# Reordering POOL's scatters, an earlier query copy and a few small copies in a sparse graph-network kernel

## The chip, the cores and the metric

The kernel runs on one core of one Trainium2 chip. The metric is the device time of one execution in microseconds, and lower is better. The kernel before took 2139.91 us, the median of three runs (2137.19 to 2143.26).

## The reference, cut to what matters

The program is a network of four graph layers on 1024 nodes with 16 batch entries of 128 features each. Layers 0, 2 and 3 are attention layers, layer 1 is a graph-attention layer without queries. About 8 of 1024 entries in each row of the adjacency matrix are set.

```python
def attention_layer(adj, h):              # layers L0, L2, L3
    Q, K, V = h @ Wq, h @ Wk, h @ Wv      # 8 heads of 16
    scores = einsum(Q, K) / sqrt(16)
    scores = where(adj == 0, -inf, scores)
    out = softmax(scores) @ V
    x = layer_norm(h + out @ Wo + bo, ln1_g, ln1_b)
    return layer_norm(x + relu(x @ W1 + b1) @ W2 + b2, ln2_g, ln2_b)

def graph_layer(x, adj):                  # layer L1
    h = x @ W
    e = leaky_relu((h @ a_src)[:, :, None] + (h @ a_dst)[:, None, :])
    att = softmax(where(adj == 0, -inf, e))
    return layer_norm(att @ h + x, ln_gamma, ln_beta)

x = L3(L2(L1(L0(x))))
```

## The kernel before

**What is computed how.** Because the graph is sparse, the kernel never builds the 1024 x 1024 scores. Its first 150 us or so turn the adjacency matrix into lists of neighbours. In each layer every node's keys and values are written as one row of a table in HBM, and a tile of 128 nodes then gathers the rows of its neighbours. The batch is cut into two groups (`g`) of eight entries, and the nodes into eight tiles (`t`) of 128, so that a layer has 16 "units" (`g`, `t`), and the program 64. `h` counts the two halves of a group.

**Parts.** A unit's neighbours are taken in chunks. One chunk is one indirect DMA of 128 rows (L968, in `gathered`). Chunks are grouped into parts. In attention layers a unit has five parts: four of two chunks and, in the fourth place, one of a single chunk, the *shared* chunk (`MIX` in the code), which collects what is left of the four groups of 32 nodes. A part's rows land in one of four gather buffers (`e`), and its gathers are put into the program four parts ahead (`AHEAD`), right after the last reader of that buffer.

**The work on a part**, for attention:

- VectorE multiplies the gathered keys by the expanded queries (L982, in `products`; 128 x 2048) and reduces over each head (L1015, in `exponentials`). ScalarE takes the exponential (L1019).
- VectorE multiplies the gathered values by the exponentials (L1043, in `weighted`). This is the last reader of the buffer `e`.
- TensorE sums the weighted rows by node, with a matrix of marks as the weights (L1059, in `marked`, called by `summed`).

For the shared chunk the first product is made by GpSimd (POOL) instead, in place, in the tile `qx` (L997, in `product_of_shared`). `qx` has a single buffer. Ahead of it `shared` copies to `qx` those rows of the expanded queries `qr` that the shared chunk needs, by two or three DMAs on SyncE's queue (SP, L946). The reduction L1015 and the product L1043 of that chunk then work on `qx`, and TensorE's sum reads it last.

**The end of a unit.** `divided` takes the sum of the exponentials (a matmul), VectorE divides (L1096, L1099), and two tails per unit (`attention_tail`, one for each half) do the output projection, the norms and the feed-forward part, mostly on TensorE and ScalarE. `finish` closes a tail. In layers L0 to L2 it stores the new state (`kept`, L575) and projects it to the next layer's table (L592, L617, L618), both by DMAs on SP. In L3 it transposes the result back into the tile `outs` on ScalarE (L660) and, after the second half, scatters it to the output by an indirect DMA on POOL (L699); the very last unit scatters its two halves separately (L693).

**The order.** The order of instructions is written out by hand; no scheduler moves them. The main loop goes over all parts. In one turn it emits, for part `i`: the product of part `i`, the sum of part `i - 2`, steps of the tails and of the next unit's queries (`others`), the scores and exponentials of part `i`, on the unit's second turn `shared(u)`, more `others`, the weighted rows of part `i - 1`, the gathers of part `i + 3`, and the product of the shared chunk of part `i + 2`. When a tail's steps come is set by a table of letters for each layer (`PLANS`), or by a pace. Each engine and each issuing queue works in the order in which it was given its instructions. In L3 a scatter comes out of one of the `others` of a unit's second turn, which puts it in POOL's queue ahead of the two gathers of the unit's last part, the product L997 and the sum of checks `seen` (L1112).

**Small weight parts.** `load_weights` loads an attention layer's weights and folds the mean and one bias into others: it subtracts a product of `W1` and `b2` from `b1` (L529, VectorE, from PSUM). `load_graph_weights` transposes the graph layer's weight matrix; VectorE copies the transpose `wgT` (L551) and two further columns (L555) out of PSUM.

```python
            if here and i == begun + 1:
                if is_attention(u):
                    shared(u)
...
                gathered(i - 1 + AHEAD)
                product_of_shared(i + 2)
```

Of the kernel before, what the change touches and what calls it, by code (L numbers as in the profile page):

```python
# [17 lines left out]
AF = mybir.ActivationFunctionType  # L18
ALU = mybir.AluOpType
# [4 lines left out]
D = 128  # L24
# [3 lines left out]
F = FF // P  # L28
# [117 lines left out]
def sparse_path(ctx: ExitStack, tc: tile.TileContext, a: dict, out: bass.AP, flag):  # L146


    nc = tc.nc
# [329 lines left out]
    w = {}  # L479
# [12 lines left out]
    def load_weights(layer):  # L492

        t = wts.tile([P, 2 * D], F32, tag="Wkv", name="Wkv")
        nc.sync.dma_start(t[:, :D], a[f"{layer}_gnn_Wk"])
        nc.sync.dma_start(t[:, D:], a[f"{layer}_gnn_Wv"])
        w[layer, "Wkv"] = t
        yield  # L500
        for name in ATTN:
            src = a[f"{layer}_gnn_{name}"]
            if name in ("Wq", "Wo", "W1"):
                t = wts.tile([P, src.shape[1]], F32, tag=name, name=name)
                nc.sync.dma_start(t, src)
            elif name == "W2":
                t = wts.tile([P, F, D], F32, tag=name, name=name)
                nc.sync.dma_start(t, src.rearrange("(f p) d -> p f d", p=P))
            elif name == "b1":
                t = wts.tile([P, F], F32, tag=name, name=name)  # L510
                with nc.allow_non_contiguous_dma(reason="a bias, once"):
                    nc.sync.dma_start(t, src.rearrange("(f p) -> p f", p=P))
            elif name.startswith("ln") or name in ("b2", "bo"):
                t = wts.tile([P, 1], F32, tag=name, name=name)
                nc.sync.dma_start(t, src.rearrange("(p o) -> p o", o=1))
            else:
                continue
            w[layer, name] = t
        yield
        centred(w[layer, "Wo"], D)  # L520
        centred(w[layer, "W2"].rearrange("p f d -> p (f d)"), F * D)
        ps = bank([P, F])
        for f in range(F):
            nc.tensor.matmul(
                ps[:, f : f + 1], w[layer, "W1"][:, f * P : (f + 1) * P], w[layer, "b2"],
                start=True, stop=True,
            )
        yield
        nc.vector.tensor_tensor(w[layer, "b1"], w[layer, "b1"], ps, ALU.subtract)  # L529
        nc.vector.tensor_tensor(w[layer, "ln1_b"], w[layer, "ln1_b"], w[layer, "b2"], ALU.add)  # L530

    wg = const.tile([P, D + 2], F32, name="wg")

    def load_graph_weights():
        for name in GAT[3:]:
            t = const.tile([P, 1], F32, name=name)
            nc.sync.dma_start(t, a[f"L1_gnn_{name}"].rearrange("(p o) -> p o", o=1))
            w["L1", name] = t

        nc.sync.dma_start(wg[:, :D], a["L1_gnn_W"])  # L540
        ends = const.tile([P, 2], F32, name="ends")
        for k, name in enumerate(("a_dst", "a_src")):
            nc.sync.dma_start(
                ends[:, k : k + 1], a[f"L1_gnn_{name}"].rearrange("(p o) -> p o", o=1)
            )
        yield
        ps = bank([P, P])
        nc.tensor.transpose(ps, wg[:, :D], ident)
        yield
        wgT = wts.tile([P, P], F32, tag="Wo", name="wgT")  # L550
        nc.vector.tensor_copy(wgT, ps)  # L551
        ps = bank([P, 2])
        nc.tensor.matmul(ps, wgT, ends, start=True, stop=True)
        yield
        nc.vector.tensor_copy(wg[:, D:], ps)  # L555
        centred(wg[:, :D], D)

    tables = {}
# [106 lines left out]
        return v.rearrange("p (o d) -> p o d", o=1).to_broadcast([P, GH, D])  # L665

    leaving = {}

    def finish(l, g, t, h, z, gain, shift, dve=False):
        if l + 1 < len(LAYERS):  # L670

            wanted[0] = True
            while held[0]:
                advance(slow)
            wanted[0] = False
            busy[0] += 1
            xn = states.tile([P, GH, P], F32, tag="xT", name="xT")
            turned(z, xn, gain, shift)
            yield "free"
            yield from project(l + 1, g, t, h, xn)  # L680
            busy[0] -= 1
            return
        xn = states.tile([P, GH, P], F32, tag="xT", name="xT")
        turned(z, xn, gain, shift, dve)
        yield
        if h == 0:
            leaving[g, t] = twos.tile([P, HF, GH, D], F32, tag="kv", name="outs")
        o = leaving[g, t]
        turned(xn, o[:, h], dve=dve)
        yield  # L690
        yield
        if (l, g, t) == units[-1]:
            nc.gpsimd.indirect_dma_start(  # L693
                out=out.rearrange("n (k c) -> (n k) c", k=GR * HF),
                out_offset=bass.IndirectOffsetOnAxis(ap=halves[:, h : h + 1], axis=0),
                in_=o[:, h].rearrange("p g d -> p (g d)"), in_offset=None,
            )
        elif h + 1 == HF:
            nc.gpsimd.indirect_dma_start(  # L699
                out=out.rearrange("n (k c) -> (n k) c", k=GR),  # L700
                out_offset=bass.IndirectOffsetOnAxis(ap=places[:, g, t : t + 1], axis=0),
                in_=o.rearrange("p h g d -> p (h g d)"), in_offset=None,
            )

    def hidden():
        return ones_.tile([P, F * GH * P], F32, tag="f1", name="f1")
# [168 lines left out]
    def is_attention(u):  # L875
        return LAYERS[units[u][0]][1] is ATTN
# [62 lines left out]
    def shared(u):  # L939

        qx[u] = queries_of_shared()
        of = [j for j, _ in QUARTERS[units[u][2]]]
        for j in sorted(set(of)):
            at = slice(32 * of.index(j), 32 * (S - of[::-1].index(j)))
            if of[: S].count(j) * 32 == at.stop - at.start:
                nc.sync.dma_start(qx[u][at], qs[u][at, j, :])  # L946
                continue
            for s in range(S):
                if of[s] == j:
                    at = slice(32 * s, 32 * s + 32)  # L950
                    nc.sync.dma_start(qx[u][at], qs[u][at, j, :])
# [36 lines left out]
    def product_of_shared(i):  # L988

        if i >= len(parts):  # L990
            return
        u, pieces = parts[i]
        if not is_attention(u) or (MIX, 0) not in pieces[0]:
            return
        own = qx[u].rearrange("p (o c) -> p o c", o=1)
        prs[i] = [own]
        nc.gpsimd.tensor_tensor(own, es[i][:, :1, :ROW], own, ALU.mult)  # L997
# [142 lines left out]
    def planned(beyond="abq"):  # L1140
        n = opening[0]
        opening[0] += 1
        for c in plan[0][n] if n < len(plan[0]) else beyond:
            if c == "q":
                aside()
                continue
            for gen in tails:
                if half_of[gen] == "ab".index(c):
                    step(gen, tails)
                    break  # L1150
# [4 lines left out]
    def others():  # L1155
        if opening[0] is not None:
            planned()
            for _ in range(eager[0]):
                advance(idle())
            return  # L1160
        pace[0] += pace[1]
        while pace[0] >= 1.0:
            advance(tails)
            pace[0] -= 1.0
        aside()
        for _ in range(eager[0]):
            advance(idle())
# [18 lines left out]
    with tc.manual_schedule():  # L1186
# [41 lines left out]
        begun = 0  # L1228
        for i in range(len(parts) + 2):
            here = i < len(parts)  # L1230
            u = parts[i][0] if here else len(units)
            if here:
                l = units[u][0]
                eager[0] = 1 if u < 2 else 0
                if i and parts[i - 1][0] != u:
                    begun = i
# [11 lines left out]
            if i > 1:  # L1248
                summed(i - 2)
                done = parts[i - 2][0]  # L1250
                if parts[i - 1 : i] == [] or parts[i - 1][0] != done:
                    closing = divided(done)
                    next(closing)
            others()
            if here:
                exponentials(i)
            if here and i == begun + 1:
                if is_attention(u):
                    shared(u)
                while loads:  # L1260
                    advance(loads)
                if u + 1 < len(units):
                    fronts.append(queries(u + 1))
                loads.append(loaded(u + 2))
                if u:
                    advance(loads)
            others()
            if 0 < i <= len(parts):
                weighted(i - 1, 0)
                if not is_attention(parts[i - 1][0]):  # L1270
                    others()
                    weighted(i - 1, 2)
                gathered(i - 1 + AHEAD)
                product_of_shared(i + 2)
                for _ in sizes:
                    pass
            if closing is not None and here:
# [25 lines left out]
                    advance(fronts)  # L1303
        while opening[0] < len(plan[0]):
            planned()
        while tails:
            advance(tails)
        for _ in closing:
# [438 lines left out]
```

## Time and profile before

| | |
|---|---|
| median of three runs | 2139.91 us |
| the profiled execution's own time | 2128.25 us |
| its span | 2126.4 us |
| TensorE (PE) busy | 1955.3 us (92%) |
| VectorE (DVE) busy | 1818.9 us (86%) |
| ScalarE (ACT) busy | 1516.5 us (71%) |
| GpSimd (POOL) busy | 1173.0 us (55%) |
| granted TensorE clock, mean | 0.973 |

The profile is of one execution. "Busy" is the time in which an engine ran an instruction; instructions that only issue a DMA on SP are not counted. A row of the groups gives the line, the engine, the operation, out<-in, the count, then the busy time, the mean of one in ns, and the idle time of the engine just ahead of it with what ended that idle time. A row of the waits gives who waited for whom, then the sum in us, the number of times and the longest. A row of the timeline gives start, length, engine, line and operation, and in brackets the idle time ahead of it. A row of the busy time by stage gives the stretch, its length, and for TensorE, its weight loads, VectorE, ScalarE and POOL the busy time and the number of instructions, then the granted clock, the busy share of the DMA engines and GB/s.

In time the program runs: lists of neighbours and first projections to about 130 us, layer L0 to about 660, L1 to about 1000, L2 to about 1530, L3 to about 2090, and the last two tails to 2126.4.

### The profile page before, as it was taken

The page shows a single profiled execution, that of the slowest core. Times are in us where ns is not written, and L with a number is a line of the kernel's source. Part 1 is how long each engine was busy: PE and PEld are TensorE (multiplying, and loading weights), DVE is VectorE, ACT ScalarE, POOL GpSimd, SP SyncE. Part 2 cuts the span into 40 slices and gives each one's busy share as a digit, 9 for nine tenths or more (in the row PEclk, how much of TensorE's full clock was granted, in tenths as well). Part 3 has the DMA queues.
Part 4 walks back from the last instruction along what each step waited for, and adds up shares of the span by engine and source line. Part 5 has one row for each costly group of instructions (what it writes and reads, how often), then busy time and mean ns, then how long its engine had stood idle before and what let it go on. Part 6 is the DMA issues. An engine that isn't in the chain of part 4 may idle for free.

```text
span 2126.4 us, 37294 instructions
## 1 busy us (share of the span) xinstructions
PE 1955.3 (92%) x13444; PEld 1240.3 (58%) x13444; DVE 1818.9 (86%) x1320; ACT 1516.5 (71%) x5043; POOL 1173.0 (55%) x747
## 2 busy tenths in 40 slices
PE   7679999999999989998899999999999999999986
PEld 6455666656666555555465665666655555555544
DVE  6977889999997576677989999999998989988983
ACT  3447878888886555555587888888887787777764
POOL 3344555555556477684555555555555666656550
PEclk8789999999999999999999999999999999999998
DMA  7988888888998799998899999999998888788960
GB/s 271 347 283 287 316 295 297 305 298 305 316 314 297 234 338 355 320 365 310 311 321 323 329 339 314 331 336 337 332 314 274 301 277 306 249 298 279 296 223 22
DMA packets 164800, 636.10 MB, mean 299 GB/s; under 512 B 34664, under 2 KB 37480, under 8 KB 116110
## 3 DMA queue, kind: packets, MB, share of 16 engines
q0 software_dynamic: 88720, 485.08, 64.6%
q1 hardware_dynamic: 75888, 148.57, 21.6%
q8 instruction: 108, 1.77, 0.3%
q14 instruction: 84, 0.69, 0.1%
HBM read 581.08 MB, written 92.34 MB: 317 GB/s over the span
## 4 chain that ended last, share of the span: by engine, by line
PE 47%; DVE 17%; DMA 14%; issue 13%; POOL 5%; ACT 4%; POOLq 0%; DVEq 0%; ACTq 0%
DMA e<-table,idx 13%; PE acc L1059 12%; DVE pr L1043 5%; PE yps L752 5%; PE ps L738 5%; PE ps L654 5%; DVE pr L982 4%; POOL e L968 4%; PE ps L583 3%; PE ps L932 3%; DVE sc L1015 3%; PE yps L756 2%; PE yps L728 2%; PE yps L727 2%; PE ps L923 2%
## 5 line engine op out<-in xcount | busy, mean ns | idle before, releaser
L968 POOL DMA_INDIRECT e<-table,idx x576 | 890.2, 1545 | 683.9 <-DVE pr L1043 417.9
L1043 DVE TENSOR_TENSOR pr<-e,ex 128x2048 f32<-128x2048 f32 x272 | 630.0, 2325 | 76.7 <-ACT ex L1019 38.4
L1059 PE MATMUL acc<-pr,marks 128*32 128x512 f32 x2200 | 442.8, 621 | 57.5 <-DVE pr L1043 43.9
L982 DVE TENSOR_TENSOR pr<-e,qr 128x2048 f32<-128x2048 f32 x192 | 440.4, 2294 | 43.1 <-ACT qr L935 21.0
L1015 DVE TENSOR_REDUCE sc<-pr 128x128 f32<-128x2048 f32 x192 | 438.9, 2286 | 6.6
L631 ACT ACTIVATE z<-yps,root 128x128 f32<-128x128 f32 x888 | 314.3, 372 | 175.7 <-PE yps L756 124.6
L1059 PEld LDWEIGHTS acc<-pr,marks 128*32 128x32 f32 x2200 | 93.9, 111 | 292.6 <-issue 204.2
L752 PE MATMUL yps<-W,f 128*128 128x128 f32 x1520 | 249.8, 282 | 7.5 <-ACT f L747 5.6
L647 ACT ACTIVATE z<-yps,rstd 128x128 f32<-128x128 f32 x888 | 252.2, 369 | 3.5
L752 PEld LDWEIGHTS yps<-W,f 128*128 128x128 f32 x1520 | 203.5, 191 | 65.4 <-ACT f L747 29.0
L935 ACT COPY qr<-ps 128x512 f32<-128x512 f32 x384 | 204.0, 600 | 16.7 <-PE ps L932 15.8
L583 PE MATMUL ps<-Wkv,xT 128*128 128x256 f32 x768 | 199.7, 406 | 15.2 <-ACT xT L662 7.4
L587 ACT COPY kv<-ps 128x512 f32<-128x512 f32 x176 | 102.6, 587 | 140.2 <-PE ps L583 120.5
L738 PE MATMUL ps<-x,W 128*128 128x512 f32 x384 | 187.0, 610 | 1.3 <-issue 0.9
L631 ACT ACTIVATION_READ_ACCUMULATOR z<-yps,root 128x1 f32 x888 | 187.4, 211 | 0.0
L583 PEld LDWEIGHTS ps<-Wkv,xT 128*128 128x128 f32 x768 | 146.1, 200 | 59.7 <-issue 15.8
L654 PE MATMUL ps<-ident,z 128*128 128x128 f32 x896 | 151.9, 286 | 20.9 <-ACT z L647 11.3
L997 POOL TENSOR_TENSOR qx<-e,qx 128x1024 f32<-128x1024 f32 x48 | 134.4, 2800 | 62.3 <-DMA qx<-qr 34.5
L747 ACT ACTIVATE f<-ps,b 128x512 f32<-128x512 f32 x190 | 127.5, 692 | 49.2 <-PE ps L738 48.0
L727 PE MATMUL yps<-Wo,oT 128*128 128x128 f32 x768 | 155.4, 285 | 2.1 <-ACT oT L660 1.9
L728 PE MATMUL yps<-centre,x 128*128 128x128 f32 x768 | 154.4, 283 | 2.1 <-ACT x L723 0.2
L932 PE MATMUL ps<-q,rep 32*128 32x512 f32 x768 | 141.3, 640 | 8.5 <-ACT q L927 7.7
(178 smaller groups left out, 2794.9 us busy)
## 6 DMA issues: line engine op xcount, KB each, us to landing
table<-kv SPq DMA_DIRECT2D x88, 512.0 KB
kept<-xT SPq DMA_DIRECT2D x96, 256.0 KB
x<-kept SPq DMA_DIRECT2D x48, 512.0 KB
qx<-qr SPq DMA_DIRECT2D x54, 256.0 KB
e<-table,idx POOLq DMA_INDIRECT x576
table<-kv SPq DMA_DIRECT2D x32, 256.0 KB
qx<-qr SPq DMA_DIRECT2D x48, 128.0 KB
qx<-qr SPq DMA_DIRECT2D x12, 384.0 KB
```

The lines of the kernel that those rows point to most:

```text
L583: nc.tensor.matmul(ps[:, k, :], x[:, i + k, :], w[LAYERS[l][0], "Wkv"], start=True, stop=True,)
L631: nc.scalar.activation(z[:, i, :], y[:, i, :], AF.Square, scale=D**-0.5, bias=root, accum_out=total[:, i : i + 1],)
L647: nc.scalar.activation(z[:, i, :], y[:, i, :], AF.Copy, scale=rstd[:, i : i + 1])
L654: nc.tensor.transpose(ps[:, i, :], z[:, i, :], ident)
L738: nc.tensor.matmul(ps, p["W1"][:, f * P : (f + 1) * P], x1.rearrange("p g n -> p (g n)"), start=True, stop=True,)
L752: nc.tensor.matmul(ps[:, i, :], f1[:, f, i * P : (i + 1) * P], p["W2"][:, f, :], start=(f == 0), stop=False,)
L932: nc.tensor.matmul(ps, rep_of(j), q[32 * j : 32 * j + 32], start=True, stop=True)
L968: nc.gpsimd.indirect_dma_start(out=es[i][:, k, :], out_offset=None, in_=tables[l, g][:, :], in_offset=bass.IndirectOffsetOnAxis(ap=idx[:, ...
L982: nc.vector.tensor_tensor(prs[i][0][:, :n, :], es[i][:, :n, :ROW], of_piece(qs[u], piece), ALU.mult,)
L1015: nc.vector.tensor_reduce(sc[:, :n, :], prs[i][0][:, :n, :].rearrange("p k (a d) -> p k a d", d=HD), mybir.AxisListType.X, ALU.add,)
L1043: nc.vector.tensor_tensor(prs[i][k0 // 2][:, :m, :].rearrange("p k (a d) -> p k a d", d=d), es[i][:, k0 : k0 + m, base : base + ROW].rearr ...
L1059: nc.tensor.matmul(outs[32 * j : 32 * j + 32], marks[:, mark, :], rhss, start=(chunk == mine[0]), stop=(chunk == mine[-1]),)
```

## The change

Three things are changed.

1. **Scatters.** In L3, `finish` no longer issues a unit's scatter where the tail stands, but leaves it in the list `ready`. The main loop issues what is in `ready` after the turn's gathers and the product of the shared chunk. What is left is issued after the loop. The two scatters of the very last unit stay as they were.
2. **Shared queries.** `shared(u)` is called on the unit's first turn, ahead of the first `others`, instead of on its second turn, after them.
3. **Small parts of the weights.** The subtraction from `b1` is done by ScalarE as two activations of one column each, and the copies of `wgT` and of the two further columns are ScalarE's.

```diff
@@ load_weights
-        nc.vector.tensor_tensor(w[layer, "b1"], w[layer, "b1"], ps, ALU.subtract)
+        for f in range(F):
+            one = w[layer, "b1"][:, f : f + 1]
+            nc.scalar.activation(one, ps[:, f : f + 1], AF.Identity, bias=one, scale=-1.0)
@@ load_graph_weights
-        nc.vector.tensor_copy(wgT, ps)
+        nc.scalar.copy(wgT, ps)
...
-        nc.vector.tensor_copy(wg[:, D:], ps)
+        nc.scalar.copy(wg[:, D:], ps)
@@ finish
+    ready = []
...
         elif h + 1 == HF:
-            nc.gpsimd.indirect_dma_start(
+            rows = o.rearrange("p h g d -> p (h g d)")
+            ready.append(lambda: nc.gpsimd.indirect_dma_start(
                 out=out.rearrange("n (k c) -> (n k) c", k=GR),
                 out_offset=bass.IndirectOffsetOnAxis(ap=places[:, g, t : t + 1], axis=0),
-                in_=o.rearrange("p h g d -> p (h g d)"), in_offset=None,
-            )
+                in_=rows, in_offset=None,
+            ))
@@ main loop
+            if here and i == begun and is_attention(u):
+                shared(u)
             others()
             if here:
                 exponentials(i)
             if here and i == begun + 1:
-                if is_attention(u):
-                    shared(u)
                 while loads:
                     advance(loads)
...
                 gathered(i - 1 + AHEAD)
                 product_of_shared(i + 2)
+                while ready:
+                    ready.pop(0)()
                 for _ in sizes:
                     pass
...
         while opening[0] < len(plan[0]):
             planned()
+        while ready:
+            ready.pop(0)()
         while tails:
             advance(tails)
```

## The prediction

> **What bounds the kernel now.** I read the page first, then the chain of waits stage by stage, then the waits, and last the timeline of one tile's pass ("unit") in the last layer. The page shows two engines near full:
>
> ```profile
> PE 1955.3 (92%) x13444; PEld 1240.3 (58%) x13444; DVE 1818.9 (86%) x1320; ACT 1516.5 (71%) x5043; POOL 1173.0 (55%) x747
> L997 POOL TENSOR_TENSOR qx<-e,qx 128x1024 f32<-128x1024 f32 x48 | 134.4, 2800 | 62.3 <-DMA qx<-qr 34.5
> ```
>
> No single engine bounds all of it. In the first layer (150 to 660 us) the chain of what ended last is nearly all TensorE; in the last layer (1600 to 2090 us) it is gathers, VectorE and POOL's L997 and L968. Busy time by stage agrees; the two rows are layer L2 (16 units) and 13 units of layer L3, from product to product:
>
> ```profile
> 1004.40:1541.00 536.60, 518.81 (x3486) 332.13 (x3486) 502.84 (x281) 427.63 (x1374) 291.75 (x177) 0.99 0.95 327
> 1614.80:2066.10 451.30, 416.34 (x2763) 255.13 (x2762) 416.48 (x222) 339.37 (x1113) 270.97 (x157) 0.98 0.84 285
> ```
>
> A unit takes 33.5 us in L2 and 34.7 us (451.3/13) in L3, though L3 has no keys and values to project and its DMA engines are busy 0.84 instead of 0.95. The waits of 1600 to 2126 us name what is peculiar to L3:
>
> ```profile
> POOL out L699 <- ACT both L1109: 105.4, 13, 23.4
> DVE sc L1015 <- POOL qx L997: 22.1, 7, 3.3
> POOL out L699 <- ACT outs L660: 8.0, 2, 4.4
> ```
>
> The scatter of the output (L699) makes POOL wait for ScalarE, and behind it in POOL's queue stand the unit's last two gathers and the product L997 that VectorE wants. One unit, POOL and then VectorE, from the timeline:
>
> ```profile
> 1675.58 1.09 POOL L699 DMA_INDIRECT out<-outs,places  x1 [7.52 <-ACT both L1109]
> 1676.97 1.01 POOL L968 DMA_INDIRECT e<-table,idx  x1 [0.30 <-issue]
> 1678.29 2.87 POOL L968 DMA_INDIRECT e<-table,idx  x1 [0.31 <-issue]
> 1681.17 2.39 POOL L997 TENSOR_TENSOR qx<-e,qx 128x1024 f32<-128x1024 f32 x1
> ```
>
> ```profile
> 1644.52 4.48 DVE L1043 TENSOR_TENSOR pr<-e,ex 128x2048 f32<-128x2048 f32 x1
> ...
> 1669.43 2.28 DVE L1043 TENSOR_TENSOR pr<-e,ex 128x2048 f32<-128x2048 f32 x1
> ...
> 1673.48 2.28 DVE L982 TENSOR_TENSOR pr<-e,qr 128x2048 f32<-128x2048 f32 x1
> 1675.80 2.29 DVE L1015 TENSOR_REDUCE sc<-pr 128x128 f32<-128x2048 f32 x1
> 1678.01 2.28 DVE L1043 TENSOR_TENSOR pr<-e,ex 128x2048 f32<-128x2048 f32 x1
> 1683.59 1.22 DVE L1015 TENSOR_REDUCE sc<-qx 128x64 f32<-128x1024 f32 x1 [3.31 <-POOL qx L997]
> ```
>
> The gathers' buffer was free at 1671.7 (end of the L1043 of 1669.43), but they were issued at 1677, after the scatter. So the product came at 1681 and VectorE stood still for 3.31 us. In other units it starts with VectorE's L1043, which then takes 4.48 us instead of 2.28 (first row). Either way the late product costs VectorE 2 to 3 us a unit.
>
> **What the Trainium skill says.** "SBUF — State Buffer", section "Who interferes with whom": a VectorE instruction with two SBUF inputs contends with a GpSimd instruction that reads SBUF, and the first keeps the shared port for its whole length; a reduction does not contend. The trace agrees: L1043 grows by 2.20 us, about the 2.36 of the product it starts with, and L1015 (one input) stays at 2.29 beside a product. "DMA: Bandwidth & Descriptors", section "SWDGE vs HWDGE vs iDMA": descriptors of POOL's DMAs are built on GpSimd itself, so they stand in POOL's order; agreed, 1.0 us each here and 2.8 when a two-input VectorE instruction runs beside them. "Perfetto Trace Analysis", section "DMA Instruction — SWDGE (GPSIMD)": the recorded end is that of descriptor generation, not of the data, so L968's end is not a landing.
>
> **Part 1: scatters behind gathers and product.** 14 units of L3 have a scatter ahead of their last two gathers (the 15th comes when the products are over). Their losses, read from VectorE's timeline: seven idle stretches before L1015, 22.1 us; seven stretched L1043 (six of 4.48 to 4.50, one of 3.18, against 2.28), 6 x 2.21 + 0.90 = 14.2 us. Sum 36.3, or 2.6 a unit.
>
> After the change POOL does gathers, product, scatter. In the unit above the gathers start near 1671.9; one takes 1.0, the other meets L982 (1673.48) and ends near 1676.6; the product could run 1676.7 to 1679.1 and stretch L1043 by 1.1. If the gathers are over before L982 starts, the product waits for L982, runs beside the reduction and costs nothing. L2, which has no scatter in this place, shows both: of 16 products none leaves VectorE idle and five stretch L1043 (0.71 to 1.35, sum 4.9), 0.30 a product. I take L2's rate: 14 x 0.30 = 4.3 left of 36.3, 32 us gained.
>
> What is late next: (a) gathered rows. VectorE's L982 waits 7.9 us for them in these 13 units; at a unit of 32.5 us the DMA share rises from 0.84 to 0.84 x 34.7/32.5 = 0.90. I allow 0.4 us a unit, 5.6 us; bounds 0 and 1.6 a unit (22 us). (b) TensorE: where L2's chain is TensorE alone, a unit takes 32.6 us (L1059 at 1447.02, 1479.64, 1512.26); L3 lacks the 16 projections (3.5 us) and has 8 more transposes (1.1): 30.2, under 32.5. (c) VectorE itself: 416.5 less 13 of the stretches, 31.0 a unit. Both allow the gain.
>
> The scatter's own 1.0 to 3.0 us now stand ahead of the next unit's first two gathers and the sum L1112. Those gathers wait for the L1043 behind the product in any case (in L2 they start 0.3 after its end), so they slip by about 1 us against L2, and against now by -2 to +3. That is inside the 0.4 of (a). Where ScalarE is late with `outs` (waits of 9 to 10 us in three units) POOL still waits, but with an already issued pair of gathers; the next pair isn't due before. **Net: -26 us** (bounds -45, with the gather waits and 7.1 us of L1096 waiting for TensorE gone too, and +10).
>
> **Part 2: `shared(u)` a part sooner.** 48 units issue the same 114 DMAs, now ahead of `kept` and `table` stores on SP. They must wait for the matmuls that read the old `qx`; those are issued just before, so in L3, where SP already waits only for them (qx at 1665.92, matmuls over at 1665.83), nothing moves. In L0 SP stands on `kept`'s wait for ScalarE and qx goes out about 4 us late: POOL waits 29.6 us for it in ten units between 150 and 650, and VectorE 9.0 (four idle spells), plus about 7 of stretched L1043. But this stage's chain is TensorE (331.7 busy of 350 us), which hides it. I take -2 us; bounds -12 and +3 (stores behind qx: they wait for later ScalarE work anyway).
>
> **Part 3: ScalarE takes small parts.** VectorE loses three additions of 0.16 us and two copies (0.28, 0.15); the wait of 1.15 us for TensorE before one addition goes: -1. ScalarE gains six activations near 0.2 us and two copies near 0.2. All but `wgT` lie in slack. `wgT` was copied by VectorE at 115.6; on ScalarE it stands behind a `kv` copy that started at 118.66 (held by a DMA) and an exponential ending 119.4. The matmul behind it on TensorE (L553, 115.92) slips to about 119.7 and with it two projections and the queries' matmul of 119.79, which VectorE awaits (8.33 us until 132.8). **+1 us**, bounds 0 and +4.
>
> **Sum.** -26 - 2 - 1 + 1 = -28 us. The profiled execution took 2128.25 us (span 2126.4); against it 2100. The median of runs is 2139.91, 11.7 above it; I carry the difference over: **2112 us**.
>
> **Rivals.**
> *More comes free (2100).* The three waits of L1096 for TensorE (7.1 us) and part of the gather waits are results of the late product and go as well: -28 - 12. For it: a unit of L3 before the first scatter took 30.9 us (products at 1539.98 and 1570.88). Against: the one before it took 35.2.
> *The product waits for its rows instead (2131).* The gather it reads may land late; the chain shows 11 to 12.8 us from its issue to the next step in seven units, for instance 1665.26 to 1677.6. Landing then, the product would still stretch L1043 by 2.1 a unit: 14 x 2.1 = 29 of 36 remain, gain 7 to 10. Against: the gathers before it move into idle DMA time, and in L2, at DMA share 0.95, only five of 16 products wait for rows (1.35 to 3.24 us).
> *Slower (2150).* The scatter, stretched by L1043 to 3.0 us, holds the next unit's first gathers (0.3 us after L1043 now, in units with a stretched L1043), and VectorE waits for them, as it does already by 0.2 to 1.5 us in ten units. At 3.3 us in 14 units that is 46, less 36, +10. It decides where the slip exceeds the gain of 2.6 a unit. Against: 0.9 us of the slip fall before VectorE frees the buffer, in most units.
>
> **How the numbers follow.** Forecast 0.58; more 0.13; rows late 0.21; slower 0.08. About 0.3% (6.4 us) is what a measurement can tell from no change: 2133.5 to 2146.3 is "the same". Forecast and "more" are faster; two thirds of "rows late" are, too; part of "slower" lies within 0.3%: faster 0.83, same 0.11, slower 0.06. The range, 2098 to 2133, runs from "more" to the weak end of "rows late".
>
> **What would show it.** Right: in L3 L1015 no longer waits for L997, L1043's mean falls from 2553 ns towards 2350, a unit from 34.7 to about 32.5, the scatter's wait shrinks. POOL's wait for qx in L0 should shrink without the stage getting shorter. Wrong: units of L3 stay over 34 with L982 waiting for rows, or products waiting for DMA.

## The result, and the profile after

The changed kernel takes 2126.53 us, the median of 16 runs (2121.49 to 2134.1); the kernel before took 2137.4 beside it, also in 16 runs. The ratio is 0.9945, with a 95% interval of 0.9931 to 0.9959: 11.8 us faster (8.8 to 14.7). The forecast was 28 us faster. The direction is right and the time lies in the range, but less than half of the gain came, and, as the experiments show, hardly any of it from the part that was to bring 26.

The profiled execution took 2124.14 us (span 2122.2). Lines were inserted further up, so L968, L982, L997, L1015, L1043 of before are L972, L986, L1001, L1019, L1047 now, the scatter is L703, and the sum of checks L1116. The page of the changed kernel, its engines and POOL's product:

```profile
PE 1967.2 (93%) x13444; PEld 1247.9 (59%) x13444; DVE 1802.1 (85%) x1315; ACT 1517.8 (72%) x5051; POOL 1174.2 (55%) x747
L1001 POOL TENSOR_TENSOR qx<-e,qx 128x1024 f32<-128x1024 f32 x48 | 147.9, 3081 | 50.5 <-DMA e<-table,idx 26.5
```

VectorE is busy for 16.8 us less, yet the end has moved by a quarter of that in this pair of traces. Busy time by stage of the changed kernel, the same 13 units of layer L3:

```profile
1605.70:2055.90 450.20, 431.79 (x2779) 264.43 (x2777) 402.36 (x222) 342.10 (x1118) 267.82 (x157) 0.98 0.81 284
```

VectorE took 416.48 us for 222 instructions before and takes 402.36 now. Most of the difference is the stretch of its weighted products, whose mean was 2553 ns before (row of the groups for these 13 units):

```profile
L1047 DVE TENSOR_TENSOR pr<-e,ex 128x2048 f32<-128x2048 f32 x52 | 120.8, 2323 | 0.4 <-ACT ex L1023 0.4
```

Of the 14.2 us of stretch that the prediction counted 2.4 are left. But the stage went only from 451.3 to 450.2 us, 34.6 us a unit where 32.5 was forecast. VectorE's idle time in it grew from 451.3 - 416.5 = 34.8 to 47.8 us. The waits of the changed kernel from 1600 to 2126 us say for what:

```profile
POOL e L972 <- DVE pr L1047: 146.7, 27, 8.1
...
DVE pr L986 <- DMA e<-table,idx: 39.8, 13, 4.3
...
POOL out L703 <- ACT both L1113: 23.2, 1, 23.2
```

VectorE's wait for POOL's product (22.1 us) has no row any more, and POOL waits for ScalarE ahead of a scatter only once, for the last one. In their place VectorE's product waits 39.8 us for gathered rows, where it waited 7.9. One unit from the timeline shows how; POOL of the changed kernel first:

```profile
1635.53 0.99 POOL L972 DMA_INDIRECT e<-table,idx  x1 [3.92 <-DVE pr L1047]
1636.82 0.99 POOL L972 DMA_INDIRECT e<-table,idx  x1 [0.30 <-DMA e<-table,idx]
1637.84 3.70 POOL L1001 TENSOR_TENSOR qx<-e,qx 128x1024 f32<-128x1024 f32 x1
1641.70 3.06 POOL L703 DMA_INDIRECT out<-outs,places  x1 [0.16 <-issue]
1645.07 2.98 POOL L972 DMA_INDIRECT e<-table,idx  x1 [0.30 <-ACT z L649]
1648.35 1.88 POOL L972 DMA_INDIRECT e<-table,idx  x1 [0.31 <-issue]
```

And VectorE of the same unit:

```profile
1641.56 2.28 DVE L1047 TENSOR_TENSOR pr<-e,ex 128x2048 f32<-128x2048 f32 x1
1643.75 1.21 DVE L1019 TENSOR_REDUCE sc<-qx 128x64 f32<-128x1024 f32 x1
1644.88 2.28 DVE L1047 TENSOR_TENSOR pr<-e,ex 128x2048 f32<-128x2048 f32 x1
1647.08 2.28 DVE L986 TENSOR_TENSOR pr<-e,qr 128x2048 f32<-128x2048 f32 x1
1649.40 2.29 DVE L1019 TENSOR_REDUCE sc<-pr 128x128 f32<-128x2048 f32 x1
1651.60 1.22 DVE L1047 TENSOR_TENSOR qx<-e,ex 128x1024 f32<-128x1024 f32 x1
1655.49 2.29 DVE L986 TENSOR_TENSOR pr<-e,qr 128x2048 f32<-128x2048 f32 x1 [2.67 <-DMA e<-table,idx]
```

POOL's product now meets the end of L986 and then a reduction, and costs VectorE nothing. Behind it the scatter starts 0.14 us after the L1047 of 1641.56 and takes 3.06 us instead of about 1: it ends 0.92 us after that product. That L1047 frees the next buffer at 1643.84. The pair of gathers for it starts only at 1645.07, after the scatter, and there it meets the next two-input products of VectorE: 2.98 and 1.88 us, so that it is issued at 1650.23, 6.4 us after the buffer was free. From the free buffer to the first use of these rows VectorE has other work of 9.0 us. The rows come at 1655.49, 11.65 us after it, and 2.67 us are lost.

The same pair in the kernel before, POOL:

```profile
1644.49 2.36 POOL L997 TENSOR_TENSOR qx<-e,qx 128x1024 f32<-128x1024 f32 x1
1649.28 1.02 POOL L968 DMA_INDIRECT e<-table,idx  x1 [2.43 <-DVE pr L1043]
1650.60 2.60 POOL L968 DMA_INDIRECT e<-table,idx  x1 [0.30 <-ACT ex L1019]
```

And the product of VectorE that uses its rows:

```profile
1658.17 2.29 DVE L982 TENSOR_TENSOR pr<-e,qr 128x2048 f32<-128x2048 f32 x1 [0.19 <-DMA e<-table,idx]
```

Its buffer was free at 1649.00 (the stretched L1043 of 1644.52), its issue over at 1653.20, 4.2 us later, and VectorE used the rows at 1658.17 after a wait of 0.19: 9.2 us after the free buffer. So in this unit the rows were just in time before, with nothing to spare; the issue slipped by 2.2 us and the wait grew by 2.5.

The other units agree. Count from the end of the pair's issue to the moment when VectorE has done its other work and is ready for the rows: in 13 of 14 units these were 4.7 to 4.9 us before, in 12 of 14 they are 2.6 us now. Before, seven units were like the one above. In six others the pair was issued as late as 6.6 to 7.6 us after its buffer, but VectorE was ready only 11.3 to 12.5 us after it, because in between it waited for POOL's product. So the wait that part 1 takes away was itself time in which these rows came. Of the 39.8 us, all but 0.3 are waits for this pair.

### The profile page after: what moved, and what is told of

It is laid out like the page before. It is cut to its first block, busy times and chain, and to the rows that moved or that the text cites. A ratio compares the mean times of both kernels' runs of the same rounds, so it can differ in the third digit from the quotient of the medians.

```text
span 2122.2 us, 37311 instructions
## 1 busy us (share of the span) xinstructions
PE 1967.2 (93%) x13444; PEld 1247.9 (59%) x13444; DVE 1802.1 (85%) x1315; ACT 1517.8 (72%) x5051; POOL 1174.2 (55%) x747
## 3 DMA queue, kind: packets, MB, share of 16 engines
q0 software_dynamic: 88720, 485.08, 64.6%
## 4 chain that ended last, share of the span: by engine, by line
PE 46%; DVE 18%; DMA 14%; issue 12%; ACT 6%; POOL 4%; POOLq 0%; SPq 0%; DVEq 0%; ACTq 0%
DMA e<-table,idx 12%; PE acc L1063 12%; DVE pr L1047 5%; DVE pr L986 5%; PE ps L656 5%; PE yps L756 5%; PE ps L742 5%; PE ps L585 4%; DVE sc L1019 4%; POOL e L972 3%; PE ps L936 2%; PE yps L760 2%; PE yps L732 2%; PE yps L731 2%; PE ps L927 2%
## 5 line engine op out<-in xcount | busy, mean ns | idle before, releaser
L972 POOL DMA_INDIRECT e<-table,idx x576 | 869.0, 1509 | 777.8 <-DVE pr L1047 519.9
L1047 DVE TENSOR_TENSOR pr<-e,ex 128x2048 f32<-128x2048 f32 x272 | 614.5, 2269 | 73.8 <-ACT ex L1023 40.2
L986 DVE TENSOR_TENSOR pr<-e,qr 128x2048 f32<-128x2048 f32 x192 | 441.9, 2302 | 86.2 <-DMA e<-table,idx 52.8
L1063 PE MATMUL acc<-pr,marks 128*32 128x512 f32 x2200 | 438.1, 609 | 34.5 <-DVE pr L1047 21.1
L1019 DVE TENSOR_REDUCE sc<-pr 128x128 f32<-128x2048 f32 x192 | 438.9, 2286 | 6.6
L1001 POOL TENSOR_TENSOR qx<-e,qx 128x1024 f32<-128x1024 f32 x48 | 147.9, 3081 | 50.5 <-DMA e<-table,idx 26.5
L936 PE MATMUL ps<-q,rep 32*128 32x512 f32 x768 | 149.5, 640 | 9.7 <-ACT q L931 8.3
```

The source lines that it names most:

```text
L972: nc.gpsimd.indirect_dma_start(out=es[i][:, k, :], out_offset=None, in_=tables[l, g][:, :], in_offset=bass.IndirectOffsetOnAxis(ap=idx[:, ...
L986: nc.vector.tensor_tensor(prs[i][0][:, :n, :], es[i][:, :n, :ROW], of_piece(qs[u], piece), ALU.mult,)
L1019: nc.vector.tensor_reduce(sc[:, :n, :], prs[i][0][:, :n, :].rearrange("p k (a d) -> p k a d", d=HD), mybir.AxisListType.X, ALU.add,)
L1047: nc.vector.tensor_tensor(prs[i][k0 // 2][:, :m, :].rearrange("p k (a d) -> p k a d", d=d), es[i][:, k0 : k0 + m, base : base + ROW].rearr ...
L1063: nc.tensor.matmul(outs[32 * j : 32 * j + 32], marks[:, mark, :], rhss, start=(chunk == mine[0]), stop=(chunk == mine[-1]),)
```

## The experiments

**The theories.** *Issue*: the scatter's own time on POOL, stretched to 3 us by VectorE's product, holds the next unit's gathers; the wait it makes cancels what part 1 gained. *Data*: the scatter's bytes compete with the gathers. *Gathers*: at a shorter unit the gathered rows bound L3 whatever the scatter does. Beside these stand the three parts, each alone. Every ratio is to the kernel before, in runs on the same chip. "Unit" is the distance of the shared chunk's reductions in L3, over 13 units of one trace: 34.71 us before, 34.72 after.

### The scatter elsewhere, thinner, or gone

Behind the next unit's first pair of gathers instead of ahead of it (to the changed kernel):

```diff
-                while ready:
+                while ready and i != begun + 1:
```

> The changed kernel, with the scatter one step further back: behind the first two gathers of the next unit (third turn of the unit) instead of ahead of them. Theory 1 (issue): in the changed kernel the scatter's 3 us of descriptor work delay the issue of that pair, and VectorE waits 44 us for its rows; behind the pair the wait falls to about 10 us in L3, a unit of L3 from 34.6 to about 32.5 us, ratio to the kernel before 0.980 to 0.985. Theory 2 (data): the scatter's 512 KB stand ahead of the pair's rows; they are behind now too, so the same. Theory 3 (the gathers bound L3 whatever stands ahead of them, the unit stays 34.6 us): ratio 0.994 as the changed kernel.

Measured: 2109.77 us, ratio 0.9862 (0.9837 to 0.9887); unit 33.55 us. VectorE waits 24.1 us for rows in L3, not about 10:

```profile
DVE pr L986 <- DMA e<-table,idx: 24.1, 16, 3.2
```

The wait has moved with the scatter: 12 of the 16 times, 18.5 us, are now waits for the unit's second pair, the one that stands behind the scatter in this kernel. Its issue is over 6.5 us after its buffer is free, where it is 5.0 us in the next kernel (medians).

Behind the single gather of the next unit's first turn:

```diff
-                while ready:
+                while ready and (i == begun or not here):
```

> The changed kernel, with the scatter on the next unit's first turn, behind its single gather and ahead of the last two. Those two had slack in the kernel before (issued 5 us late without a wait of VectorE for them). Theories 1 and 2: no gather that VectorE needs soon stands behind it; wait for rows about 6 us, a unit about 32.3 us, ratio 0.978 to 0.984. But the pair and the product L1001 stand behind 1 to 3 us of scatter, so L1047 may be stretched by up to 1 us a unit (then 0.985). Theory 3: 0.994.

Measured: 2093.45 us, ratio 0.98 (0.9778 to 0.9822), 43 us faster than the kernel before and the lowest ratio of all; unit 32.61 us. The waits of this kernel from 1600 to 2126 us:

```profile
POOL qx L1001 <- DMA e<-table,idx: 22.1, 8, 4.4
...
DVE pr L986 <- DMA e<-table,idx: 4.6, 6, 1.5
```

POOL in one of its units:

```profile
1638.11 1.03 POOL L972 DMA_INDIRECT e<-table,idx  x1 [2.56 <-DVE pr L1047]
1639.44 2.60 POOL L972 DMA_INDIRECT e<-table,idx  x1 [0.30 <-ACT z L649]
...
1654.19 2.80 POOL L972 DMA_INDIRECT e<-table,idx  x1 [2.63 <-DVE pr L1047]
1657.29 1.03 POOL L703 DMA_INDIRECT out<-outs,places  x1 [0.31 <-issue]
1660.91 1.02 POOL L972 DMA_INDIRECT e<-table,idx  x1 [2.59 <-DVE pr L1047]
```

VectorE's product that frees the pair's buffer, and its reduction at the time of the scatter:

```profile
1635.56 2.28 DVE L1047 TENSOR_TENSOR pr<-e,ex 128x2048 f32<-128x2048 f32 x1
...
1656.15 2.29 DVE L1019 TENSOR_REDUCE sc<-pr 128x128 f32<-128x2048 f32 x1
```

The pair is over at 1642.04, 4.2 us after its buffer (1637.84), as in the unit of the kernel before. The scatter runs beside the reduction, takes 1.03 us, and POOL still stands idle for 2.59 us behind it, until VectorE frees the next buffer: here the scatter is really hidden. The wait for rows falls from 39.8 to 4.6 us. Some of POOL's products now wait for rows themselves (22.1 us), and L1047 is stretched by 9.7 us in all.

The scatters at the changed place, but thin:

```diff
+THIN = 128
...
-            rows = o.rearrange("p h g d -> p (h g d)")
+            rows = o.rearrange("p h g d -> p (h g d)")[:, :THIN]
...
-                out=out.rearrange("n (k c) -> (n k) c", k=GR),
+                out=out.rearrange("n (k c) -> (n k) c", k=GR * (ROW // THIN)),
```

> The changed kernel with the 15 scatters at the same place, but each writes only the first 128 of 1024 values of a row, and to another place (an eighth of the bytes; the rest of the output is left out). [...]Theory 1 (issue): descriptor work stays near 3.0 us, the wait for rows stays near 44 us, ratio 0.994. Theory 2 (data): the wait falls below 20 us, ratio below 0.987.

Measured: 2123.67 us, ratio 0.9945 (0.9921 to 0.9968), the changed kernel's own; unit 35.00 us. The lines of the scatter in the two kernels, the changed one and then the thin one (count: shortest, median and longest in ns, first and last start):

```profile
L703 POOL DMA_INDIRECT out<-outs,places x15: 992/3056/3063, 1608.4 to 2086.5; - x15
```

```profile
L704 POOL DMA_INDIRECT out<-outs,places x15: 1004/3069/3081, 1603.6 to 2089.0; - x15
```

The wait of the thin one:

```profile
DVE pr L987 <- DMA e<-table,idx: 40.3, 11, 5.3
```

POOL's queue moved 6.9 MB less in this trace (485.08 to 478.19), which is seven eighths of 15 scatters of 512 KB. With an eighth of the data the scatter holds POOL just as long, and the rows are waited for just as long. The data theory falls.

The scatters left out:

```diff
-            ready.append(lambda: nc.gpsimd.indirect_dma_start(
-                out=out.rearrange("n (k c) -> (n k) c", k=GR),
...
+            ready.clear()
```

> The changed kernel with the 15 scatters left out (only the last unit's two remain, so most of the output is not written). Theories 1 and 2: no wait for rows beyond 6 us, unit of L3 about 32.2 us, ratio 0.978 to 0.983; this is the most that any place of the scatter can bring. Theory 3: VectorE waits for rows all the same, ratio 0.990 or more.

Measured: 2102.06 us, ratio 0.9828 (0.9799 to 0.9857); unit 32.70 us; wait for rows 11.0 us. The gathers allow a unit of 32.7 us, so they don't bound L3 at 34.7; the third theory falls. TensorE, busy for 431.8 of 450.2 us in the changed kernel's L3, doesn't bound it there either: its work is the same with the scatters behind the single gather, at a unit of 32.61.

Of the 11.0 us of waiting, where at most 6 were expected, 4.2 fall in one unit. There the pair starts 1.1 us after its buffer is free instead of 0.3, with no scatter ahead of it:

```profile
1838.13 3.15 POOL L968 DMA_INDIRECT e<-table,idx  x1 [3.37 <-issue]
```

It meets the product that VectorE began at 1838.10, and the pair is over 6.4 us after its buffer. So here the late start costs the same without a scatter. That this kernel isn't faster than the one with the scatters behind the single gather isn't explained; the two intervals overlap.

### The parts alone

Part 1 alone (the kernel before with the diff of `finish` and the two loops over `ready`):

```diff
+            ready.append(lambda: nc.gpsimd.indirect_dma_start(
...
                 product_of_shared(i + 2)
+                while ready:
+                    ready.pop(0)()
```

> Part 1 alone: the scatters behind gathers and product, shared queries and small parts as before. If the whole gain of 0.55% is part 1's (its first unit with a scatter, 6 us earlier in the profile), ratio 0.994. If part 1 only trades one wait for another in L3, 0.998 to 1.0.

Measured: 2124.35 us against 2126.11, ratio 0.9993 (0.9979 to 1.0007). Its waits from 1600 to 2126 us:

```profile
DVE pr L984 <- DMA e<-table,idx: 38.3, 11, 4.8
```

VectorE's wait for the shared product is gone and the stretch of its weighted products in L3 falls from 14.2 to 2.0 us, which frees about 34 us. Its wait for rows grows by 30.4 us (7.9 to 38.3), and two of its products of keys (L984) are stretched by 4.1. Within the interval, part 1 is worth nothing.

Part 2 alone:

```diff
+            if here and i == begun and is_attention(u):
+                shared(u)
             others()
...
-                if is_attention(u):
-                    shared(u)
```

> Part 2 alone: the shared queries' copy one turn sooner. My prediction: -2 us (0.999), since TensorE bounds L0. Rival: it brings the larger part of the gain, 0.996 or less, with L0 shorter by 5 us or more.

Measured: 2119.34 us, ratio 0.9969 (0.9957 to 0.9981): 6.6 us faster, more than the 2 us predicted.

Part 3 alone (all three edits of `load_weights` and `load_graph_weights`):

```diff
-        nc.vector.tensor_tensor(w[layer, "b1"], w[layer, "b1"], ps, ALU.subtract)
...
+            nc.scalar.activation(one, ps[:, f : f + 1], AF.Identity, bias=one, scale=-1.0)
...
-        nc.vector.tensor_copy(wgT, ps)
+        nc.scalar.copy(wgT, ps)
```

> Part 3 alone: small weight parts on ScalarE. My prediction: 0 us (between -1 and +4), 1.000. The matmul behind the copy of wgT slips by 3 to 4 us near 116 us; rival: VectorE's fewer waits at the start bring 2 us or more, 0.999.

Measured: 2120.43 us, ratio 0.9978 (0.9961 to 0.9995): 4.7 us faster, where 0 was predicted.

The whole change beside them, unaltered:

> The changed kernel itself on the same chip, to set beside its parts: 0.9945 (0.993 to 0.996). If the parts add up, the three ratios' distances from 1 sum to 0.0055.

Measured: 2112.66 us, ratio 0.9949 (0.9929 to 0.9968), 10.8 us. The parts' distances from 1 add up to 0.0007 + 0.0031 + 0.0022 = 0.0060, the whole's is 0.0051: within the interval the sum of the parts is the whole.

### Where parts 2 and 3 gain

Part 2 in the first layer only, and in L2 and L3 only:

```diff
+            if here and i == begun and is_attention(u) and l == 0:
+                shared(u)
...
-                if is_attention(u):
+                if is_attention(u) and not (l == 0):
                     shared(u)
```

(with `l > 0` in both places in the other kernel)

> The kernel before, with the shared queries' copy one turn sooner in L0 only. Part 2 alone gave 0.9969. If its gain lies in L0 (VectorE's 9 us of waits and 7 us of stretched products there end on the chain after all), 0.997 here. If TensorE hides it, as I predicted, 0.999 to 1.000.

> The kernel before, with the shared queries' copy one turn sooner in L2 and L3 only. I predicted that nothing moves there: 1.000. Rival: the gain of part 2 lies in L2, where the copy went out behind the stores of the new state: 0.997.

Measured: 2119.52 us, ratio 0.9962 (0.9946 to 0.9978), for the first layer; 2127.65 us, 1.0005 (0.9988 to 1.0023), for the late ones. So the gain of part 2 lies in L0. The waits of the late-layer kernel from 150 to 650 us keep the old order's rows:

```profile
POOL qx L997 <- DMA qx<-qr: 42.3, 12, 7.9
...
DVE sc L1015 <- POOL qx L997: 9.8, 3, 4.3
```

In the kernel with the early copies in L0 the first is left with 3.0 us and the second is gone:

```profile
POOL qx L997 <- DMA qx<-qr: 3.0, 3, 2.3
```

The ends of L0 agree on the two chips on which the parts ran: its last shared reduction starts at 654.1 to 655.6 us in the three traces with the early copies there, at 661.0 to 666.3 in the five without. (Single traces can mislead: in the pair of the result the changed kernel has 660.4 and the kernel before 657.5.)

Part 3's edits apart: the subtraction only, and the two copies only (each the lines of part 3's diff that concern it).

> Of part 3 only the subtraction from b1 on ScalarE. In the trace of before VectorE waits 6.68 us for TensorE ahead of L529 at 763.6, in the graph layer, which my working overlooked; ScalarE waits 1.87 us there in the trace of part 3 alone. If that wait is on the chain, 0.9970 to 0.9975 (-5 to -6.5 us); if it is hidden, 0.9995 to 1.000.

> Of part 3 only the two copies of the graph layer's weights on ScalarE. In the trace of part 3 alone the product that waits for the queries' copies starts at 134.99 instead of 132.83. So +1 to +2 us, 1.0005 to 1.001, as predicted; rival: nothing or a gain, 0.999.

Measured: 2120.32 us, ratio 0.9961 (0.9946 to 0.9976), for the subtraction; 2126.4 us, 1.0006 (0.9989 to 1.0024), for the copies. The gain is the subtraction's. From the last shared reduction of L0 to the first of L2 it is 335.3 us in its trace and 341.8 to 344.1 in the three others of the same chip, so the gain shows in L1. VectorE in the kernel before, in layer L1, where the weights of L2 are made:

```profile
756.75 0.19 DVE L1028 SCALAR_TENSOR_TENSOR sc<-sc 128x32 f32<-128x32 f32 x1
763.62 0.16 DVE L529 TENSOR_TENSOR b<-b,ps 128x2 f32<-128x2 f32 x1 [6.68 <-PE ps L524]
763.70 0.16 DVE L530 TENSOR_TENSOR ln_b<-ln_b,b 128x1 f32<-128x1 f32 x1
763.77 2.28 DVE L1043 TENSOR_TENSOR pr<-e,ex 128x2048 f32<-128x2048 f32 x1
```

VectorE stood still for 6.68 us before an addition of 0.16 us, because TensorE came late to four small matmuls, and behind it in VectorE's queue stood a weighted product. VectorE at the same place with the subtraction on ScalarE:

```profile
762.60 0.19 DVE L1030 SCALAR_TENSOR_TENSOR sc<-sc 128x32 f32<-128x32 f32 x1
762.71 0.24 DVE L532 TENSOR_TENSOR ln_b<-ln_b,b 128x1 f32<-128x1 f32 x1
762.88 2.28 DVE L1045 TENSOR_TENSOR pr<-e,ex 128x2048 f32<-128x2048 f32 x1
```

The wait for TensorE is gone; VectorE waits 1.11 us for gathered rows just ahead of these lines. ScalarE waits for the same matmuls in the kernel with part 3 alone, but only 1.87 us, for two activations of 0.41 us together:

```profile
764.31 0.41 ACT L531 ACTIVATE b<-ps,b 128x1 f32<-128x1 f32 x2 [1.87 <-PE ps L524]
```

The copies did what was expected at their place: the product that waits for the next unit's queries starts at 135.45 in the copies' trace instead of 132.83. Their cost in time, forecast as +1, is below what these runs can tell from nothing.

## Why the prediction was right or wrong

**Part 1, the gain: right.** The product no longer waits behind the scatter; it meets L986 and a reduction. The idle 22.1 us are gone, 14.2 us of stretch fell to 2.4 (L2's rate had given 4.3), and L1047's mean fell to 2323 ns (forecast 2350). A unit of 32.5 us is what is left without the scatter's harm: 32.61 and 32.70 were measured with it behind the single gather and without it. The closeness is partly luck, for there the weighted products are stretched by 9.7 and 7.8 us, not by 4.3.

**Part 1, the price: wrong; this is the step that failed.** The prediction put the slip of the next unit's first gathers at about 1 us against L2 and took it to lie "inside the 0.4 of (a)", the waits for rows. The slip at the start came as forecast: in 13 of 14 units the pair starts 1.2 us after its buffer is free, about 1 us later than L2's 0.3. Two things were mis-sized. First, the slip doubles on its way. In all 14 units the scatter starts beside a two-input product of VectorE and takes 2.92 to 3.06 us; its late end puts the pair beside the next two products, and in 12 units the issue is over 6.4 us after the free buffer instead of 4.2. Second, there was no slack for it. VectorE already waited 0.2 to 1.5 us for this pair in six units, and in six units the pair had come in time only because VectorE itself was held up by the late product. The term was put at 5.6 us for L3; the wait for rows grew by 31.9 (7.9 to 39.8) and ate the 34 or so that were freed. The measured worth of part 1 is -1.8 us in the medians (-4.5 to +1.5 by the interval), not -26.

**The rivals.** The mechanism is that of the rival named "Slower", given 0.08: the stretched scatter holds the next unit's first gathers. It priced 3.3 us a unit, 46 in all; 39.8 us of waiting, 7.9 of which was there before, made a draw of it and not a loss. "More comes free" is ruled out for this order, though its 2100 us, 0.981 of the kernel before, is reached with the scatter elsewhere (0.98). The rival "rows late" had the product L1001 wait for its rows: with the changed order it does so in L3 for 4.4 us, with the scatter behind the pair, behind the single gather or left out for 17.0, 22.1 and 25.9 us. So that wait is real, and shows once the scatter is out of the way; that it alone sets the unit of 32.6 us isn't shown. The prediction had a sign of it but misread it: of the five waits for rows that it put in L2, those of 3.24 and 1.35 us belong to the first two products of L3 (1539.98 and 1570.88), ahead of any scatter; in L2 itself the trace puts three down to rows, 2.3 to 2.9 us. The reason against "Slower", that 0.9 us of the slip fall before the buffer is free, was true and not enough: in the unit shown 2.1 of the scatter's 3.06 us do, but the pair then starts 0.19 us after the next product (1645.07, 1644.88) instead of ahead of it.

**Part 2: place right, size off.** Nothing moves in L2 and L3, as forecast. In L0 -2 us was forecast, because TensorE's chain hides it; -6.6 and -8.1 us were measured, inside the bounds of -12 and +3. VectorE's wait for POOL's product there goes from 9.0 to 0 us and the stretch of its products from about 7 to about 3, so of some 13 us half or more reached the end. So TensorE hid less than the prediction read from the chain of waits. Through which waits the gain reaches the end isn't settled.

**Part 3: one row overlooked.** For the subtraction the prediction counted one wait, 1.15 us. The same line had another, 6.68 us, in L1. The copies' +1 is neither shown nor contradicted (-2.3 to +5.1 us by the interval). Net 0 was forecast, -4.7 measured.

**The sum.** -26 - 2 + 0 became -1.5 - 6.6 - 4.7 (from the ratios). That the time landed within the range was luck: two small parts brought more than was thought, while the large one brought nothing that can be told from noise.

## What to carry to other kernels

When an issue is moved back in a queue, the place it goes to has to be priced as carefully as the place it leaves: look for a point where the queue stands idle after it anyway, and where no neighbour stretches it. A wait that is short but comes back in many units marks work that is just in time, with no slack to hide a slip; and a wait that a change removes may be the slack of something else. And for an instruction that moves to another engine, list every one of its occurrences with the wait ahead of it, not its line's mean duration: an addition of 0.16 us held VectorE for 6.68.

## What the runs showed of the hardware

- An indirect DMA's issue on POOL takes about 1.0 us (0.97 to 1.05 in L2 and L3 of the two traces of the result), unless it starts beside a VectorE product with two inputs in SBUF; then it takes up to 3.06 us. It isn't slowed in proportion but held: in L2 and L3 of the changed kernel's trace, all 117 issues that start during such a product end 0.86 to 0.93 us after the product does, whether 0.6 or 2.15 us of it were left. In the unit shown the scatter ends at 1644.76 and its product at 1643.84, the gathers at 1648.05 and 1650.23 and theirs at 1647.16 and 1649.36.
- The amount of data didn't matter: 128 values in each of 128 rows took 3069 ns in the median and 1004 at the shortest, 1024 values 3056 and 992.
- The stretch repeats along a queue. The scatter's 3.06 us put the next gather beside another product, which made it 2.98, and the one after it 1.88; starting 0.95 us sooner against the buffer's release, the same pair took 1.02 and 2.60. So a slip of 0.95 us at its start grew to 2.2 at its end.
